# Attention of a fused kernel: where the softmax reciprocals are spread, and how x1 for the residual is made

## The chip, the cores and the metric

The kernel runs on one core of a Trainium2 chip. Time is the device time of one execution in microseconds, the median of several runs. A profile is one execution taken by the hardware profiler; its span runs from the first to the last instruction. The engines are TensorE (PE in the profile; PEld is its loading of weights), VectorE (DVE), ScalarE (ACT), GpSimd (POOL) and SyncE (SP), whose work here is to issue transfers. Each engine works through its own instructions in order. All arithmetic is in float32.

## The reference

Four layers run over 8 sequences (batches) of 512 rows by 512 features: a finite-difference grid step, a transformer layer with conditioning, an expert MLP with layer normalization, and a gated low-rank correction. The change lies in the second, whose attention half is

```python
emb = silu(sin_emb(timestep)) @ W_ada + b_ada
scale, shift = split(emb)                      # one row of 512 each per batch
x = ln(src) * (1.0 + scale) + shift            # x1
q, k, v = x @ Wq + bq, x @ Wk + bk, x @ Wv + bv    # 16 heads of 32
scores = q @ k.T / sqrt(32) + attention_bias   # masked with -inf
ctx = softmax(scores) @ v
x = x + (ctx @ Wo + bo)
```

Softmax is used as exp(s - max) whose weighted sum over v is divided by its own sum. So each of the 16 heads of each row needs one reciprocal, and the residual needs x1 in rows.

## The kernel before, in words

**Stages.** The grid step of batch 0 runs first (to about 75 us of the profile), then attention of all 8 batches with the grid steps of batches 1 to 7 woven in (to about 1105 us), then the MLP stage. A tile has 128 partitions; the 512 rows of a batch are taken as 4 groups r of 128 rows, the 512 features as 4 chunks c of 128, which are 4 heads each.

**Units.** Attention is a loop (L1124 on) over 128 units (b, c, r): batch, four heads, 128 rows. Within a batch t = 4c + r counts them from 0 to 15. Three units are in work at once: `now` gets its softmax, `old` (one unit back) has its weights turned by 128x128 transposes on TensorE (`turned`, L1032), and for `two` (two units back) `values` (L1055) multiplies with v, once per two row groups. `scores` (L1003) of the next unit come last. The order on each engine is the order in which this loop records the calls; `pin` fixes it. Loads that are not pinned can be placed elsewhere by the scheduler.

**Filling.** Between these steps `fill` (L927) gives each t some other matmuls: projections q and k of this batch (t = 0, 1, 4, 5, 8, 9), the output projection `o_block` of the batch before (t = 2, 3, 6, 7), and from t = 9 on the first work of the next batch: `x1_in` (L601) turns its normalized rows `xt` by TensorE and applies scale and shift, which in the turned form are one number per partition; then q, k, v of it. `x1_back` (L617) makes rows of x1 again: four transposes (tile `xb`, PSUM) and an add of `bo` on VectorE (L622), into `xt`. It runs at t = 11 to 14, for batch 0 at t = 2, 3, 4 and 7. `o_block` later adds the attention's result to `xt`.

**Softmax and its division.** `softmax` (L1014) adds the scores to the negative bias and takes the minimum in one VectorE instruction, and ScalarE's exponential leaves the sums, `sums`, 4 heads per unit. At the end of each unit `inverse` (L1070) takes the reciprocal of `old`'s sums on VectorE and ScalarE copies each over the 32 features of its head (`rw`, 128x128). When two's r is 3 (t = 5, 9, 13, and t = 1 of the next batch), `divide` (L1077) turns the four `rw` tiles on TensorE (tile `rb`), ScalarE copies the result out of PSUM (`rbs`), and VectorE multiplies `ctx` by it into `ct` (L1087). PSUM tag `tr`, two buffers, is shared by `turned`, `x1_in`, `x1_back` and `divide`.

**Queues.** SP issues nearly all loads in program order, each after the buffers it writes are free. `load_bias` (L982) brings a unit's bias three units ahead, two halves of 512 KB; GpSimd adds the mask to it (`add_mask`, L994, line L998) one unit ahead. `grid_loads` (L729) brings coefficients and rows for the grid step of a later batch; most of their bytes come at t = 6 and 7. `grid_gate` (L741) makes GpSimd wait, once a unit, until VectorE's last grid operation is done. `x1d` stores a batch's finished rows (1 MB) at t = 9 of the next batch. `rows32` and `spread` (L1415, L1429) of the MLP stage already move rows through DRAM: VectorE transposes 32x32 blocks, one transfer writes them (`td`), eight reads bring them back in another order.

Of the kernel before, what the change touches and what calls it, by code (L numbers as in the profile page):

```python
# [11 lines left out]
F32 = mybir.dt.float32  # L12
# [4 lines left out]
ALU = mybir.AluOpType  # L17
# [3 lines left out]
NB = 8  # L21
S = 512
D = 512
P = 128
R = 4
NH = 16
HD = 32
FF = 2048
NJ = FF // P
KC = D // P  # L30
RK = 32
# [8 lines left out]
def fused_kernel(ctx: ExitStack, tc: tile.TileContext, a: dict):  # L40
    nc = tc.nc

    const = ctx.enter_context(tc.tile_pool(name="const", bufs=1))
    small = ctx.enter_context(tc.tile_pool(name="small", bufs=4))
    xp = ctx.enter_context(tc.tile_pool(name="xp", bufs=1))


    ident = const.tile([P, P], F32, name="ident")
# [116 lines left out]
    w = {}  # L165
# [30 lines left out]
    def load_late():  # L196
# [3 lines left out]
    wl3 = const.tile([P, KC, RK], F32, name="wl3")  # L200
    x1d = [dram.tile([P, R, D], F32, name=f"x1d_{b}") for b in range(NB)]
    first = attention_stage(
        tc, a, small, xp, xt, x_home, x1d, grid, ident, sc1, shift, io, wo8, w, (bqk, bvc, bo),
        g2, mhalf, load_w, load_late,
    )
    mlp_stage(tc, a, small, xp, io, wo8, x1d, ident, eidx, sigs, layernorm, rstd_of, phalf, wl3, g2, b1, first)
# [336 lines left out]


def attention_stage(
    tc, a, small, xp, xt, x_home, x1d, grid, ident, sc1, shift, io, wo8, w, rows,
    g2, mhalf, load_w, load_late,
):

# [9 lines left out]
    with ExitStack() as ctx:  # L559
# [9 lines left out]
        def tp(out, src):  # L569
            pin(nc.tensor.transpose(out, src, ident))  # L570
# [46 lines left out]
        def x1_back(b, r):  # L617
            tr = ps.tile([P, KC, P], F32, name=f"xb_{b}_{r}", tag="tr", bufs=2)
            for c in range(KC):
                tp(tr[:, c, :], x1s[b, c][:, r::R])  # L620
            pin(
                nc.vector.tensor_tensor(  # L622
                    xt[b][:, r, :], tr.rearrange("p c f -> p (c f)"), bo, ALU.add
                )
            )

        def block(out, lhsT, rhs):

# [298 lines left out]
        def fill(b, t):  # L927

            n = b + 1
            jobs = []  # L930
            if b == 0:
                if t == 0:
                    homes = (("m", 1), ("tr", 2), ("tr", 2), ("ctx", 1))
                    for m in range(4):
                        jobs.append(v_block(0, m, *homes[m]))
                        jobs.append(grid_early(j) for j in (m + 3,))
                    jobs.append(grid_early(7) for _ in range(1))
                    jobs.append(mask_out(0, r) for r in (2, 3))
                elif t == 1:
                    jobs.append(add_bv() for _ in range(1))  # L940
                elif t in (2, 3, 4, 7):
                    jobs.append(x1_back(0, (2, 3, 4, 7).index(t)) for _ in range(1))
            if n == NB:
                if t == 0:
                    head["fill"] = halves(b)
                jobs.append(
                    next(head["fill"], None)
                    for _ in range({0: 2, 7: 2, 8: 2, 11: 2, 12: 2, 13: 0, 14: 2, 15: 0}.get(t, 1))
                )
            elif t in (0, 4, 8):  # L950
                jobs.append(q_block(b, t // 4 + 1))
            elif t in (1, 5, 9):
                turn = (lambda c: x1_in(n, c)) if t == 9 else None
                jobs.append(k_block(b, t // 4 + 1, turn=turn))
            elif t in (2, 3, 6, 7):
                if b:
                    jobs.append(o_block(b - 1, (2, 3, 6, 7).index(t)))
            elif t == 11:
                jobs.append(q_block(n, 0))
            elif t == 13:  # L960
                jobs.append(k_block(n, 0))
            else:
                jobs.append(v_block(n, (10, 12, 14, 15).index(t)))
            if n < NB:
                if t in (11, 12, 13, 14):
                    jobs.append(x1_back(n, t - 11) for _ in range(1))
                if t >= 12:
                    jobs.append(load_mask(n, t - 12) for _ in range(1))
            elif t == 8:
                jobs.append(head_stats() for _ in range(1))  # L970
            elif t in (10, 11):
                jobs.append(head_norm(r) for r in (2 * t - 20, 2 * t - 19))
            elif t in (13, 15):
                jobs.append(head_turn(c) for c in (t - 13, t - 12))
            for j in jobs:
                yield from j
# [26 lines left out]
        def scores(b, c, r):  # L1003
            for i in range(4):
                s = ps.tile([P, S], F32, name=f"s_{b}_{c}_{r}_{i}", tag=f"s{i}")
                o = i * HD
                mm(
                    s, qs[b, c][o : o + HD, r * P : (r + 1) * P], ks[b, c][o : o + HD, :],
                    True, True,
                )  # L1010
                ss[i] = s
            sums[b, c, r] = pp.tile([P, 4], F32, name=f"sums_{b}_{c}_{r}", tag="sums", bufs=8)

        def softmax(b, c, r, u):  # L1014

            bt = bias[b, c, r, u]
            for i in range(2):
                h = 2 * u + i
                mn = small.tile([P, 1], F32, name=f"mn_{b}_{c}_{r}_{h}", tag=f"mn{h}")
                pin(  # L1020
                    nc.vector.tensor_tensor_reduce(  # L1021
                        bt[:, i, :], ss[h], bt[:, i, :], -1.0, 3.0e38, ALU.add, ALU.min, mn
                    )
                )
                pin(
                    nc.scalar.activation(  # L1026
                        bt[:, i, :], bt[:, i, :], AF.Exp, bias=mn, scale=-1.0,
                        accum_out=sums[b, c, r][:, h : h + 1],
                    )
                )  # L1030

# [35 lines left out]
                        k == 0, k == KC - 1,  # L1067
                    )

        def inverse(b, c, r):  # L1070
            rs = small.tile([P, 4], F32, name=f"rs_{b}_{c}_{r}", tag="rs")
            pin(nc.vector.reciprocal(rs, sums.pop((b, c, r))))
            rw = pp.tile([P, 4, HD], F32, name=f"rw_{b}_{c}_{r}", tag="rw", bufs=4)
            pin(nc.scalar.copy(rw, rs[:, :, None].to_broadcast([P, 4, HD])))
            sums["w", b, c, r] = rw

        def divide(b, c):  # L1077
            rb = ps.tile([P, R, P], F32, name=f"rb_{b}_{c}", tag="tr", bufs=2)
            for r in range(R):
                tp(rb[:, r, :], sums.pop(("w", b, c, r)).rearrange("p h d -> p (h d)"))  # L1080
            rbs = pp.tile([P, S], F32, name=f"rbs_{b}_{c}", tag="rbs", bufs=1)
            pin(nc.scalar.copy(rbs, rb.rearrange("f r p -> f (r p)")))

            tag, bufs = (("gq", 2), ("gc", 3))[c // 2] if b == NB - 1 else ("ct", 5)
            ct = pp.tile([P, S], F32, name=f"ct_{b}_{c}", tag=tag, bufs=bufs)
            pin(
                nc.vector.tensor_tensor(  # L1087
                    ct, ctxs.pop((b, c)).rearrange("f r p -> f (r p)"), rbs, ALU.mult
                )
            )  # L1090
            cts[b, c] = ct

        def drain(jobs):
            for _ in jobs:
                pass
# [28 lines left out]
        for i in range(n + 2):  # L1124
            now = units[i] if i < n else None
            old = units[i - 1] if 1 <= i <= n else None
            two = units[i - 2] if i >= 2 else None
            jobs = fill(now[0], 4 * now[1] + now[2]) if now else iter(())
            grid_gate(i)
            if i + 1 < n:  # L1130
                add_mask(*units[i + 1])
            grid_step(i - 1, grid_pow)
            pair = two and two[2] % 2 == 1
            if pair:
                values(two[0], two[1], two[2] // 2)
            for u in range(2):
                if old:
                    turned(*old, u)
                if now:
                    softmax(*now, u)  # L1140
                next(jobs, None)
            drain(jobs)
            split = pair and two[2] == R - 1
            if split:
                grid_step(i, lambda n, j: grid_sums(n, j, late=False))
                divide(two[0], two[1])
            if old:
                inverse(*old)
            if i + 3 < n:
                load_bias(*units[i + 3])  # L1150
            if now and now[0] and now[1:] == ((2, 1) if now[0] < NB - 1 else (3, 3)):
                nc.sync.dma_start(x1d[now[0] - 1], xt[now[0] - 1])
            if now and now[0] == NB - 1:
                head_load(4 * now[1] + now[2])
            grid_step(i, lambda n, j: grid_sums(n, j, early=not split))
            grid_step(i, grid_loads)
            if i + 1 < n:
                scores(*units[i + 1])
# [893 lines left out]
```

## Time and profile before

| | |
|---|---|
| Time, median of 3 runs | 2699.4 us (2698.77 to 2700.58) |
| Profiled execution, its own time | 2699.88 us |
| Span of that profile | 2698.1 us |
| Busy: PE, DVE, POOL, ACT | 2659.8, 1925.3, 1479.1, 1009.5 us |
| `tr` transposes (L570) in 75 to 1080 us | x2016, 277 ns each |
| `rb`, `xb` transposes (L570) there | x124 at 278 ns, x128 at 284 ns |
| `rw` copies (L1074, ACT) there | x126 at 292 ns |
| `rbs` copies (L1082, ACT) there | x31 at 571 ns |
| `rs` reciprocals (L1072, DVE) there | x126 at 168 ns |
| Mask additions (L998, POOL) there | x254 at 2140 ns |

How to read the lines shown below: a group has line, engine, operation, tile written and tiles read, sizes, how many, then busy time and mean ns of one, then idle time before them and what ended it. A timeline line has its start and length in us. Several instructions of a kind that follow each other are one line. Neighbouring matmuls overlap in the records, so their starts tell more than their lengths.

### The profile page before, as it was taken

How to read it: one execution, taken by the hardware profiler on the slowest of the kernel's cores; microseconds unless marked ns; L12 is line 12 of the kernel's file. 1: busy time of each engine (PE TensorE's matmuls, PEld its weight loads, DVE VectorE, ACT ScalarE, POOL GpSimd, SP SyncE). 2: the span in 40 equal slices, each digit the busy share in tenths (PEclk: the TensorE clock that was granted, in tenths of full speed). 3: DMA queues.
4: the chain of work that ended last, by engine and by line, in shares of the span. 5: the costliest groups of instructions: out<-in, count | busy, mean ns of one | idle time of the engine just before them, and what ended most of it. 6: DMA issues, size and time to landing. Idle time of an engine off the chain costs nothing.

```text
span 2698.1 us, 39602 instructions
## 1 busy us (share of the span) xinstructions
PE 2659.8 (99%) x14310; PEld 1972.4 (73%) x14310; DVE 1925.3 (71%) x3602; ACT 1009.5 (37%) x2157; POOL 1479.1 (55%) x1090
## 2 busy tenths in 40 slices
PE   7999999999999999999999999999999999999998
PEld 4455555555555555788888888888888888888887
DVE  7888888888888756576666656656556765666665
ACT  2566767676676766212212211211111211211211
POOL 3455555555555655366566465555555555555553
PEclk9999999999999999999999999999999999999999
DMA  8765757666676544644453553455335445346321
GB/s 310 247 217 179 242 182 245 194 230 220 197 242 193 171 150 137 197 146 115 138 156 98 162 146 100 146 155 152 123 118 184 127 151 190 125 146 199 121 97 45
DMA packets 218720, 451.39 MB, mean 167 GB/s; under 512 B 27192, under 2 KB 54400, under 8 KB 209438
## 3 DMA queue, kind: packets, MB, share of 16 engines
q1 hardware_dynamic: 214714, 438.12, 48.9%
q0 software_dynamic: 3360, 10.68, 2.9%
q8 instruction: 114, 1.87, 0.3%
q14 instruction: 80, 0.66, 0.1%
q10 hardware_dynamic: 452, 0.07, 0.0%
HBM read 390.04 MB, written 54.57 MB: 165 GB/s over the span
## 4 chain that ended last, share of the span: by engine, by line
PE 95%; DVE 3%; DMA 1%; issue 0%; SPq 0%; ACT 0%; ACTq 0%; POOL 0%; DVEq 0%; POOLq 0%
PE u L1195 29%; PE y L1195 29%; PE tr L570 8%; PE s L567 6%; PE ctx L567 5%; PE o L567 4%; PE pq L567 4%; PE pk L567 4%; PE pv L567 4%; PE l L251 1%; PE rb L570 1%; PE xb L570 1%; DVE x L697 0%; DMA a<-in_A 0%; DVE bt L1021 0%
## 5 line engine op out<-in xcount | busy, mean ns | idle before, releaser
L998 POOL TENSOR_TENSOR bt<-bt,mk 128x1024 f32<-128x1024 f32 x256 | 542.4, 2140 | 58.2 <-DMA bt<-in_bias 52.5
L1195 PE MATMUL y<-wo,act 128*128 128x256 f32 x2560 | 566.5, 380 | 0.0
L1195 PEld LDWEIGHTS y<-wo,act 128*128 128x128 f32 x2560 | 484.4, 190 | 71.9 <-issue 6.7
L1026 ACT ACTIVATE bt<-bt,mn 128x512 f32<-128x512 f32 x512 | 365.7, 716 | 81.4 <-DVE mn L1021 80.5
L570 PEld LDWEIGHTS tr<-ident,bt 128*128 128x128 f32 x2048 | 228.7, 141 | 145.4 <-issue 113.5
L1021 DVE CUSTOM_DVE_ANT_0 bt<-s,bt 128x512 f32<-128x512 f32 x512 | 330.8, 683 | 1.3 <-PE s L567 1.3
L1195 PE MATMUL u<-bt,wi 128*128 128x256 f32 x1440 | 330.5, 379 | 0.0
L1201 DVE TENSOR_TENSOR act<-u,u 128x512 f32<-128x512 f32 x256 | 173.1, 684 | 200.8 <-PE u L1195 132.6
L1195 PEld LDWEIGHTS u<-bt,wi 128*128 128x128 f32 x1440 | 273.5, 190 | 37.2
L570 PE MATMUL tr<-ident,bt 128*128 128x128 f32 x2048 | 274.2, 277 | 4.2 <-DVE x L622 1.7
L1195 PE MATMUL u<-tb,ws 128*128 128x256 f32 x1024 | 242.2, 379 | 0.0
L1053 ACT COPY pt<-tr 128x512 f32<-128x512 f32 x306 | 172.9, 582 | 158.8 <-PE tr L570 155.6
L1195 PE MATMUL y<-t,s 128*128 128x256 f32 x1024 | 227.8, 380 | 0.0
L1204 POOL TENSOR_TENSOR t<-wo,t 128x512 f32<-128x512 f32 x64 | 107.3, 1700 | 203.1 <-PE y L1195 203.1
L1051 DVE COPY pt<-tr 128x512 f32<-128x512 f32 x206 | 141.7, 688 | 107.4 <-PE tr L570 99.2
L1195 PEld LDWEIGHTS u<-tb,ws 128*128 128x128 f32 x1024 | 194.3, 190 | 26.6 <-DVE tb L1201 0.2
L1195 PEld LDWEIGHTS y<-t,s 128*128 128x128 f32 x1024 | 194.0, 190 | 26.1
L1559 ACT ACTIVATE act<-act,b 128x512 f32<-128x512 f32 x128 | 82.9, 711 | 293.0 <-DVE act L1201 293.0
L1559 ACT ACTIVATE act<-act,bi 128x512 f32<-128x512 f32 x128 | 83.8, 712 | 282.6 <-DVE act L1201 282.6
L1578 ACT COPY u<-u 128x512 f32<-128x512 f32 x64 | 36.4, 569 | 391.3 <-PE u L1195 273.1
L567 PE MATMUL s<-kt,qt 32*128 32x512 f32 x1024 | 177.1, 642 | 1.8 <-DVE mn L1021 0.9
L1201 DVE TENSOR_TENSOR x<-y,x 128x512 f32<-128x512 f32 (+1 forms) x97 | 64.7, 680 | 154.0 <-PE y L1195 103.6
(326 smaller groups left out, 4229.2 us busy)
## 6 DMA issues: line engine op xcount, KB each, us to landing
bt<-in_bias SPq DMA_DIRECT2D x256, 512.0 KB
wo<-in_W SPq DMA_DIRECT2D x32, 1024.0 KB
wi<-in_Wi SPq DMA_DIRECT2D x32, 1024.0 KB
wo<-in_Wo_e SPq DMA_DIRECT2D x32, 1024.0 KB
wi<-in_W SPq DMA_DIRECT2D x28, 1024.0 KB
td<-tt SPq DMA_DIRECT2D x22, 1024.0 KB
bt<-td SPq DMA_DIRECT2D x176, 128.0 KB
gq<-coef_q SPq DMA_DIRECT2D x21, 512.0 KB
```

The costliest lines, as they stand in the source:

```text
L567: pin(nc.tensor.matmul(out, lhsT=lhsT, rhs=rhs, start=start, stop=stop))
L570: pin(nc.tensor.transpose(out, src, ident))
L998: nc.gpsimd.tensor_tensor(bt, bt, mask[b, r][:, None, :].to_broadcast([P, 2, S]), ALU.add)
L1021: nc.vector.tensor_tensor_reduce(bt[:, i, :], ss[h], bt[:, i, :], -1.0, 3.0e38, ALU.add, ALU.min, mn)
L1026: nc.scalar.activation(bt[:, i, :], bt[:, i, :], AF.Exp, bias=mn, scale=-1.0, accum_out=sums[b, c, r][:, h : h + 1],)
L1051: pin(nc.vector.tensor_copy(pt[:, :, r % 2, :], tr))
L1053: pin(nc.scalar.copy(pt[:, :, r % 2, :], tr))
L1195: pin(nc.tensor.matmul(out, lhsT=lhsT, rhs=rhs, start=start, stop=stop))
L1201: pin(nc.vector.tensor_tensor(out, x, y, op))
L1204: pin(nc.gpsimd.tensor_tensor(out, x, y, op))
L1559: nc.scalar.activation(acts[g][:, k, :], acts[g][:, k, :], func, bias=bi[:, j : j + 1])
L1578: pin(nc.scalar.copy(u1, p[0]))
```

## The change

Reciprocals: sums of all four units of (b, c) go to one tile of 4 heads by 4 row groups. After the fourth, one reciprocal writes 32 columns (the 16 twice), VectorE transposes them in 32x32 blocks, SP writes 16 KB to DRAM and reads it back four times with broadcast, so that each head's row of 512 reciprocals lies on its 32 partitions. `divide` multiplies by that tile, with its columns taken in the order in which they lie. `inverse` is called when old's r is 3, ahead of the rest of the unit's filling; `divide` stays where it was, one unit later.

x1 of batches 1 to 7: once, at t = 5 and 6 of batch 0, `rows_out` turns scale (which already holds the 1) and shift by four transposes each, adds `bo` to the second and stores them as rows in DRAM. At t = 8 `rows_in` brings the next batch's two rows, broadcast to 128 partitions; the second goes to `bo` itself. GpSimd multiplies (t = 10 to 13) and VectorE adds (t = 11 to 14), in place on the normalized rows. Batch 0 keeps `x1_back`.

```diff
+        ghd = dram.tile([2, NB, D], F32, name="ghd")
+        rows1 = {}
+        def rows_out(i):
+            tr = ps.tile([NB, KC, P], F32, name=f"gh_{i}", tag="tr", bufs=2)
+            for c in range(KC):
+                tp(tr[:, c, :], (sc1, shift)[i][:, c, :])
+            t = pp.tile([NB, D], F32, name=f"ghs_{i}", tag="ct", bufs=5)
+            v = tr.rearrange("b c f -> b (c f)")
+            if i:
+                pin(nc.vector.tensor_tensor(t, v, bo[0:NB, :], ALU.add))
+            else:
+                pin(nc.vector.tensor_copy(t, v))
+            pin(nc.sync.dma_start(ghd[i], t))
+        def rows_in(n):
+            rows1[n] = pp.tile([P, D], F32, name=f"gh_{n}", tag="gh", bufs=1)
+            for i, t in enumerate((rows1[n], bo)):
+                pin(nc.sync.dma_start(t, ghd[i, n : n + 1, :].to_broadcast([P, D])))
+        def x1_scale(n, r):
+            v = xt[n][:, r, :]
+            pin(nc.gpsimd.tensor_tensor(v, v, rows1[n], ALU.mult))
+        def x1_shift(n, r):
+            v = xt[n][:, r, :]
+            pin(nc.vector.tensor_tensor(v, v, bo, ALU.add))
...
                 elif t in (2, 3, 4, 7):
                     jobs.append(x1_back(0, (2, 3, 4, 7).index(t)) for _ in range(1))
+                elif t in (5, 6):
+                    jobs.append(rows_out(t - 5) for _ in range(1))
...
             if n < NB:
+                if t == 8:
+                    jobs.append(rows_in(n) for _ in range(1))
+                if t in (10, 11, 12, 13):
+                    jobs.append(x1_scale(n, t - 10) for _ in range(1))
                 if t in (11, 12, 13, 14):
-                    jobs.append(x1_back(n, t - 11) for _ in range(1))
+                    jobs.append(x1_shift(n, t - 11) for _ in range(1))
...
-            sums[b, c, r] = pp.tile([P, 4], F32, name=f"sums_{b}_{c}_{r}", tag="sums", bufs=8)
+            if r == 0:
+                sums[b, c] = pp.tile([P, 4, R], F32, name=f"sums_{b}_{c}", tag="sums", bufs=3)
...
-        def inverse(b, c, r):
-            rs = small.tile([P, 4], F32, name=f"rs_{b}_{c}_{r}", tag="rs")
-            pin(nc.vector.reciprocal(rs, sums.pop((b, c, r))))
-            rw = pp.tile([P, 4, HD], F32, name=f"rw_{b}_{c}_{r}", tag="rw", bufs=4)
-            pin(nc.scalar.copy(rw, rs[:, :, None].to_broadcast([P, 4, HD])))
-            sums["w", b, c, r] = rw
+        rd = [dram.tile([P, RK], F32, name=f"rd_{i}") for i in range(2)]
+        def inverse(b, c):
+            rs = pp.tile([P, 2, NH], F32, name=f"rs_{b}_{c}", tag="rs", bufs=2)
+            sm = sums.pop((b, c)).rearrange("p h r -> p (h r)")
+            pin(nc.vector.reciprocal(rs, sm[:, None, :].to_broadcast([P, 2, NH])))
+            rt = pp.tile([P, 2 * NH], F32, name=f"rt_{b}_{c}", tag="rt", bufs=2)
+            pin(nc.vector.transpose(rt, rs.rearrange("p u x -> p (u x)")))
+            d = rd[c % 2]
+            pin(nc.sync.dma_start(d, rt))
+            rbs = sums["b", b, c] = pp.tile([P, S], F32, name=f"rbs_{b}_{c}", tag="rbs", bufs=1)
+            rows = d.rearrange("(a u h r) j -> u h a (r j)", u=2, h=4, r=R)[0]
+            for h in range(4):
+                pin(
+                    nc.sync.dma_start(
+                        rbs[h * HD : (h + 1) * HD, :].rearrange("d (a x) -> d a x", x=P),
+                        rows[h : h + 1].to_broadcast([HD, P // RK, P]),
+                    )
+                )
 
         def divide(b, c):
-            rb = ps.tile([P, R, P], F32, name=f"rb_{b}_{c}", tag="tr", bufs=2)
-            for r in range(R):
-                tp(rb[:, r, :], sums.pop(("w", b, c, r)).rearrange("p h d -> p (h d)"))
-            rbs = pp.tile([P, S], F32, name=f"rbs_{b}_{c}", tag="rbs", bufs=1)
-            pin(nc.scalar.copy(rbs, rb.rearrange("f r p -> f (r p)")))
+            rbs = sums.pop(("b", b, c))
...
                 nc.vector.tensor_tensor(
-                    ct, ctxs.pop((b, c)).rearrange("f r p -> f (r p)"), rbs, ALU.mult
+                    ct.rearrange("f (r a j) -> f r a j", r=R, j=RK),
+                    ctxs.pop((b, c)).rearrange("f r (a j) -> f r a j", j=RK),
+                    rbs.rearrange("f (a r j) -> f r a j", r=R, j=RK), ALU.mult,
                 )
...
                 next(jobs, None)
+            if old and old[2] == R - 1:
+                inverse(*old[:2])
             drain(jobs)
             split = pair and two[2] == R - 1
             if split:
                 grid_step(i, lambda n, j: grid_sums(n, j, late=False))
                 divide(two[0], two[1])
-            if old:
-                inverse(*old)
```

In the built program SP's stores of `x1d` stand, at t = 8, between the write of the reciprocals and their reads.

More of the change, by code (lines that the diff above doesn't have):

```diff
@@ L202, in fused_kernel @@
     first = attention_stage(
-        tc, a, small, xp, xt, x_home, x1d, grid, ident, sc1, shift, io, wo8, w, (bqk, bvc, bo),
+        tc, a, small, dram, xp, xt, x_home, x1d, grid, ident, sc1, shift, io, wo8, w, (bqk, bvc, bo),
         g2, mhalf, load_w, load_late,
@@ L545, in attention_stage @@
 def attention_stage(
-    tc, a, small, xp, xt, x_home, x1d, grid, ident, sc1, shift, io, wo8, w, rows,
+    tc, a, small, dram, xp, xt, x_home, x1d, grid, ident, sc1, shift, io, wo8, w, rows,
     g2, mhalf, load_w, load_late,
@@ L1027, in softmax @@
                         bt[:, i, :], bt[:, i, :], AF.Exp, bias=mn, scale=-1.0,
-                        accum_out=sums[b, c, r][:, h : h + 1],
+                        accum_out=sums[b, c][:, h, r : r + 1],
                     )
```

## The prediction

> **What bounds the kernel now.** I read the page's engine sums and its chain first, then one batch of the attention stage by windows, then the timeline of the places that the diff touches.
>
> ```profile
> PE 2659.8 (99%) x14310; PEld 1972.4 (73%) x14310; DVE 1925.3 (71%) x3602; ACT 1009.5 (37%) x2157; POOL 1479.1 (55%) x1090
> PE u L1195 29%; PE y L1195 29%; PE tr L570 8%; PE s L567 6%; PE ctx L567 5%; PE o L567 4%; PE pq L567 4%; PE pk L567 4%; PE pv L567 4%; PE l L251 1%; PE rb L570 1%; PE xb L570 1%; DVE x L697 0%; DMA a<-in_A 0%; DVE bt L1021 0%
> ```
>
> TensorE sets the time; the removed transposes (`rb`, `xb`) stand in its chain with about 1% each. One batch of attention:
>
> ```profile
> core 0: us, PE busy (x) PEld busy (x) DVE busy (x) ACT busy (x) POOL busy (x), PEclk, DMA share, GB/s
> 502.22:628.00 125.78, 125.53 (x817) 69.19 (x816) 109.84 (x236) 87.59 (x209) 71.59 (x52) 1.00 0.65 212
> ```
>
> TensorE is full (125.5 of 125.8 us), VectorE second with 109.8 (87%), so about 16 us of TensorE's time could go before VectorE's sum binds. The edit takes under 5 a batch. The clock is 1.00 here and gives nothing.
>
> **What leaves TensorE.** The groups say how many; a duration of 277 ns overlaps its neighbours, so I price a removal by starts of neighbours with and without it.
>
> ```profile
> L570 PE MATMUL xb<-ident,x 128*128 128x128 f32 x128 | 20.7, 284 | 1.0 <-ACT pt L1053 1.0
> L570 PE MATMUL rb<-ident,rw 128*128 128x128 f32 x124 | 19.2, 278 | 1.8 <-DVE pt L1051 1.0
> ```
> ```profile
> 508.68 1.88 PE L567 MATMUL pk<-x,Wk 128*128 128x512 f32 x4
> 510.39 0.60 PE L570 MATMUL rb<-ident,rw 128*128 128x128 f32 x4
> 510.93 1.14 PE L567 MATMUL s<-kt,qt 32*128 32x512 f32 x8
> ...
> 517.33 2.27 PE L567 MATMUL s<-kt,qt 32*128 32x512 f32 x8
> ...
> 548.92 1.88 PE L567 MATMUL pv<-Wv,x 128*128 128x512 f32 x4
> 550.74 1.14 PE L567 MATMUL s<-kt,qt 32*128 32x512 f32 x8
> ...
> 557.19 1.88 PE L567 MATMUL pq<-x,Wq 128*128 128x512 f32 x4
> 558.91 0.63 PE L570 MATMUL xb<-ident,x 128*128 128x128 f32 x4
> 559.47 1.14 PE L567 MATMUL s<-kt,qt 32*128 32x512 f32 x8
> ```
>
> Without either, projection to scores takes 550.74 - 548.92 = 1.82 us. With `rb` 2.25, so 0.43 each; with `xb` 2.28, so 0.46 each. Of 32 divides, 31 lie in the flow: 13.3 us. `x1_back` stays for batch 0, so 28 go: 12.9 us.
>
> **A second gain, on VectorE.** The scores at 517.33 take 2.27 us where others take 1.14: TensorE waits 1.13 us for late VectorE. What made it late in that unit:
>
> ```profile
> 510.26 1.22 DVE L697 TENSOR_TENSOR ga<-ga,gf 128x1024 f32<-128x1024 f32 x1
> 512.37 0.69 DVE L1087 TENSOR_TENSOR ct<-ctx,rbs 128x512 f32<-128x512 f32 x1 [0.88 <-ACT rbs L1082]
> ```
>
> `divide` waits 0.88 us for ScalarE's copy of `rb`. With `rbs` loaded early that wait goes, and one small reciprocal (0.09 start to start): 0.97 instead of 0.43, so 0.54 more. It recurs at t = 1 and t = 5 while the grid work of a next batch is there, 13 times: 7.0 us. Gains together: 33.2.
>
> **What is added, and where it lies.**
> - `rows_out`: two sets of four transposes on TensorE at 0.54 (the `rb` slot): 1.1 us, once.
> - VectorE loses 128 reciprocals (start to start 0.09: 11 us) and 28 `x1_back` adds, and gets 32 reciprocals, 32 transposes of 128x32 and 28 `x1_shift` adds. The new small ones I put at 0.17 each, as the reciprocal's row has it (a 128x512 transpose takes 0.70): 32 x 0.34 = 11. A wash.
> - ScalarE loses 128 copies `rw` and 32 `rbs`. It is 70% busy in the batch; I count nothing beyond the 0.88 above.
> - GpSimd gets 28 `x1_scale`, 1.1 us by half of L998's 2.14, up to 1.7 by L1204's 128x512. They follow the mask addition of the next unit and lie in GpSimd's idle time (43% of the batch); `x1_shift` comes one unit later.
> - `x1_shift` now reads two SBUF tiles where `x1_back` read PSUM. The row: a VectorE product that starts while the mask addition runs to 551.4 takes 1.88 instead of 1.22.
>
> ```profile
> 550.60 1.88 DVE L697 TENSOR_TENSOR gc<-gc,gf 128x1024 f32<-128x1024 f32 x1
> ```
>
> [...] By the row, 0.66. But VectorE's 0.7 us wait for `xb` before each add (18.3 us over 23, L622) goes, so I take 0, with ends -7 and +7 on the path.
>
> **The round trip through DRAM.** SP, in program order, gets per block of four heads: a 16 KB write that waits for VectorE, then four 64 KB reads that wait for the write; the bias, grid and mask loads of that unit stand behind them. `rows_in` adds two 256 KB broadcasts to seven units (t = 8). In all 12 MB more on a queue that moves 27 MB a batch; it is their place that counts. Nearest are the same steps of the MLP stage: 1 MB out, then reads with as many pieces (128, of 1 KB; here 512 B).
>
> ```profile
> 1175.47 0.34 SPq L1432 DMA_DIRECT2D td<-tt  x1
> 1179.33 3.66 SPq L1439 DMA_DIRECT2D bt<-td  x8
> 1184.05 0.81 ACT L1461 ACTIVATE bt<-bt,g 128x512 f32<-128x512 f32 x1 [17.93 <-DMA bt<-td]
> ```
>
> Write: 1179.33 - 1175.81 = 3.5 us, of which 1.05 MB at 384 GB/s (the window below) are 2.7, leaving 0.8 for a small one. Reads: 4.7 from first issue to use. With 0.35 on VectorE and 0.4 of issue: 6.3 us. [...] Time available, from the end of the softmax of t = 4 (502.07) to where `ct` could begin (511.4): 9.3 us; t = 0 to 1 has 9.4, t = 12 to 13 about 10. [...]
>
> [...]
>
> ```profile
> 527.69 1.13 SPq L714 DMA_DIRECT2D gq<-coef_q  x2
> 535.71 1.23 DVE L697 TENSOR_TENSOR gq<-gq,gf 128x1024 f32<-128x1024 f32 x1 [0.40 <-DMA gq<-coef_q]
> ...
> 535.70:541.00 5.30, 5.30 (x39) 3.35 (x29) 4.68 (x10) 3.14 (x8) 3.99 (x3) 1.00 1.03 384
> ```
>
> The second `gq` landed 7 us after its issue. From 527.7 to 535.7 some 2.0 MB moved (254 GB/s), so about 0.6 MB beyond the 1.4 that `gq` needed. Ahead of the small write stand two bias halves, `x` and `gc`, 2.1 MB, of which 1.5 remain: 3.9 us at 384 GB/s, until 539.6. [...] `ct` can begin at 544.8: VectorE waits 0.3 to 3 us. I take 2, nearer the upper end because `x1d` does stand there in the built program's order; VectorE has 0.5 to give (its wait at 548.7), so TensorE loses 1.5 six times: 9 us. If all is hidden, 0. The bias halves behind land about 4 us before the softmax that uses them (GpSimd adds the mask at 547.2, VectorE reads at 555.1); that cover gone would cost what they are late.
>
> [...]
>
> **The sum**, against the profiled execution of 2699.9 (span 2698.1 and 1.8 around it): 33.2 - 1.1 - 9.0 - 2.3 = 20.8, so 2679.1; it stood 0.5 over the runs' median of 2699.4, so 2679.
>
> **Rivals.** (1) All four round trips hidden: 29.8 gained, 2670; with whole slots saved (0.54 and 0.56) 2663. For it: 0.3 us is the lower end of that wait. [...] (3) On the other side: the wait at t = 9 is long. Six batches, each costing (wait - 0.5); with 29.8 to lose the sign turns at 5.5 us of wait, reads landing after 550.3. At 7 us it costs 39, time 2709. For it: DMA share 1.01 from 533 to 544, and `x1d` between write and reads; against: the backlog counted gives 548 at the latest. That the edit does nothing is excluded, since 240 transposes leave a full engine.
>
> **Chances.** Forecast case (wait of 1 to 3 us) 0.50, hidden 0.20, the middle 0.12, long wait 0.18. A measurement of this kernel tells about 0.2% (5.4 us) from no change; half of the middle case lies within it, with the tails of its neighbours: faster 0.73, same 0.09, slower 0.18. The forecast's own range is 2670 to 2687. The range for eight in ten goes from 2663 to 2705, leaving out most of case 3.
>
> **What would show it.** Groups `rb` gone and `xb` x16; a batch of 121 to 123 us; the long scores at t = 1 and 5 back near 1.3 us; `ct` waiting on DMA only at t = 9, by 1 to 3 us, in six batches; the first `o` block waiting some 4 us at the end of attention; the MLP stage as before. Wrong if `ct` waits on DMA at all t, if GpSimd waits for bias inside batches 1 to 5, or if a batch stays at 125.8.

## The result, and the profile after

The changed kernel takes 2711.7 us (median of 5 runs, 2707.7 to 2715.6) against 2699.4 (5 runs, 2698.8 to 2702.4): ratio 1.0045, 95% interval 1.0033 to 1.0056. It is 12.3 us slower, where 20 us faster was forecast. The profiled execution took 2707.7 us, the shortest of its runs, with a span of 2705.8: 7.7 us over the span before, so the trace can account for 7.7 of the 12.3 us.

The engine sums and the chain that ended last, from the page of the changed kernel:

```profile
PE 2638.5 (98%) x14078; PEld 1941.9 (72%) x14078; DVE 1979.6 (73%) x3540; ACT 960.1 (35%) x1997; POOL 1529.3 (57%) x1118
PE 82%; DVE 8%; DMA 6%; SPq 1%; issue 1%; ACT 1%; POOL 0%; ACTq 0%; DVEq 0%; POOLq 0%
PE u L1243 29%; PE y L1243 28%; PE tr L570 6%; PE s L567 4%; PE o L567 4%; PE ctx L567 3%; PE pq L567 3%; DVE bt L1057 2%; PE pk L567 2%; DMA rd<-rt 2%; DVE x L726 2%; PE pv L567 2%; DMA mu<-in_mask 1%; DVE pt L1087 1%; PE l L251 1%
```

TensorE is busy 21.3 us less than before, as the edit promised; the span is longer all the same, so about 29 us of TensorE's time are new idle time. The chain, which was TensorE almost alone, now goes through VectorE (8%) and through two transfers: the 16 KB write `rd` and the mask load `mu`. The chain of the kernel before, by engine:

```profile
PE 95%; DVE 3%; DMA 1%; issue 0%; SPq 0%; ACT 0%; ACTq 0%; POOL 0%; DVEq 0%; POOLq 0%
```

Where in a batch? The starts of the scores of each unit t, after minus before, say it. Over t = 0 to 10 each of batches 1 to 6 gains 2.8 us (batch 3: from 5.45 behind to 2.60 behind). From t = 10 to the next t = 0, batches 0 to 5 lose 5.9, 4.7, 4.0, 4.1, 3.8 and 4.1 us; batch 6, which prepares no grid step, gains 0.8. At the end of attention the kernel is 5.3 us behind, the last divide makes it 7.7, and the MLP stage keeps that to the end. Engine busy times, first over one batch's length (from t = 5 of batch 3, as in the batch line of the prediction, with its columns), then over t = 10 to 15 of batch 3 alone:

```profile
506.63:633.64 127.01, 122.17 (x786) 64.70 (x785) 117.67 (x229) 81.04 (x189) 78.94 (x56) 1.00 0.67 223
546.93:597.35 50.42, 45.72 (x290) 23.65 (x289) 47.99 (x88) 28.00 (x67) 33.58 (x22) 1.00 0.71 233
```

The same stretch, t = 10 to 15, of the kernel before:

```profile
544.33:590.67 46.34, 46.34 (x309) 26.16 (x308) 39.63 (x92) 30.75 (x75) 26.23 (x18) 1.00 0.66 211
```

TensorE was full there with 46.34 of 46.34 us. Now VectorE is busy 47.99 of 50.42 us, 8.4 more than before with four instructions fewer, and TensorE waits.

What VectorE's instructions cost there, from its groups between 200 and 960 us (batches 1 to 5), after:

```profile
L726 DVE TENSOR_TENSOR x<-x,gq 128x1022 f32<-128x1022 f32 x22 | 39.2, 1784 | 0.2
L654 DVE TENSOR_TENSOR x<-x,bo 128x512 f32<-128x512 f32 x24 | 33.5, 1397 | 0.0
L726 DVE TENSOR_TENSOR x<-x,gg 128x1024 f32<-128x1024 f32 x12 | 21.8, 1815 | 0.0
L726 DVE TENSOR_TENSOR e<-e,e 128x8 f32<-128x8 f32 x10 | 14.4, 1437 | 0.3
```

and before:

```profile
L697 DVE TENSOR_TENSOR x<-x,gq 128x1022 f32<-128x1022 f32 x22 | 26.4, 1201 | 0.2
L622 DVE TENSOR_TENSOR x<-xb,bo 128x512 f32<-128x512 f32 x25 | 17.2, 689 | 13.6 <-PE xb L570 13.6
L697 DVE TENSOR_TENSOR x<-x,gg 128x1024 f32<-128x1024 f32 x11 | 14.9, 1352 | 0.0
L697 DVE TENSOR_TENSOR e<-e,e 128x8 f32<-128x8 f32 x10 | 1.7, 167 | 0.3
```

The add of `bo` takes 1.40 us instead of 0.69, the grid's product `x<-x,gq` 1.78 instead of 1.20, and a product of 128x8 elements, `e<-e,e`, 1.44 instead of 0.17. These instructions handle as many elements as before; they stand and wait. What for shows when they are sorted by what GpSimd does meanwhile. Before, none of the 22 `x<-x,gq` met a mask addition, and each took 1.19 to 1.22 us. After, the 12 that met neither a mask addition nor `x1_scale` took 1.21 to 1.23 us, the 10 that met one 2.28 to 3.14. The adds of the kernel before, which read one operand from PSUM (`xb`), took 0.68 to 0.69 us each, 4 of the 25 with a mask addition beside them. So what waits is VectorE's work with both operands in SBUF, beside GpSimd's work on SBUF; the texts below call this "ports", which is a name alone: what the two engines share is not shown. The timelines of batch 3 show it. VectorE:

```profile
548.70 0.69 DVE L1133 TENSOR_TENSOR ct<-ctx,rbs 128x512 f32<-128x512 f32 x1 [0.51 <-DMA rbs<-rd]
...
555.31 3.85 DVE L726 TENSOR_TENSOR e<-e,e 128x8 f32<-128x8 f32 x2
...
564.53 1.77 DVE L654 TENSOR_TENSOR x<-x,bo 128x512 f32<-128x512 f32 x1
566.22 2.28 DVE L726 TENSOR_TENSOR x<-x,gq 128x1022 f32<-128x1022 f32 x1
```

GpSimd in the same time:

```profile
554.90 4.23 POOL L1033 TENSOR_TENSOR bt<-bt,mk 128x1024 f32<-128x1024 f32 x2 [4.11 <-DMA bt<-in_bias]
559.09 2.32 POOL L650 TENSOR_TENSOR x<-x,gh 128x512 f32<-128x512 f32 x1
...
561.53 4.22 POOL L1033 TENSOR_TENSOR bt<-bt,mk 128x1024 f32<-128x1024 f32 x2
565.71 1.71 POOL L650 TENSOR_TENSOR x<-x,gh 128x512 f32<-128x512 f32 x1
```

`e<-e,e` ends at 559.16, when the mask addition ends (559.13). The add of `bo` begins at 564.53 while the next mask addition runs, and ends at 566.30, 0.6 us after it; `x<-x,gq`, issued behind it, stands while `x1_scale` runs until 567.4, and ends 1.1 us later, nearly the 1.2 it takes alone. In the kernel before, `grid_gate` kept the two engines mostly apart: a mask addition began when VectorE's last grid operation was done, ran while VectorE read scores from PSUM, and was over before most of its next grid work. At t = 12 of batch 3 `x<-x,gq` ended at 561.65, the mask addition ran from 561.88 to 566.1, and the next `x<-x,gq` began at 567.14. GpSimd there:

```profile
561.73 0.19 POOL L746 TENSOR_TENSOR gate<-x 128x1 f32<-128x1 f32 x1 [2.62 <-DVE x L697]
561.88 4.23 POOL L998 TENSOR_TENSOR bt<-bt,mk 128x1024 f32<-128x1024 f32 x2
```

Two things broke that. `x1_scale` stands behind the mask additions and runs into the grid work. And the mask addition of t = 10 comes late, here by 4.11 us of waiting for bias. SP's queue shows why:

```profile
536.95 0.32 SPq L1116 DMA_DIRECT2D rd<-rt  x1
537.31 0.43 SPq L1200 DMA_DIRECT2D x1d<-x  x1
544.04 2.63 SPq L1121 DMA_DIRECT2D rbs<-rd  x4
546.71 0.43 SPq L646 DMA_DIRECT2D gh<-ghd  x1
547.18 0.43 SPq L646 DMA_DIRECT2D bo<-ghd  x1
547.72 3.22 SPq L1022 DMA_DIRECT2D bt<-in_bias  x4
```

SP stands for 6.3 us, from the store to the first read, until the write has landed; then come the four reads and two row loads, and only then the bias. It takes both: GpSimd waits for bias once in each of batches 1 to 5, 4.1 to 5.6 us each time; before it did so in none of them, and in two runs below, one without the row loads and one with them elsewhere, its waits there are under 1 us each. `ct` itself waits 0.51 us. Who else waits, over the whole span, after (us in total, times, longest):

```profile
POOL bt L1033 <- DMA bt<-in_bias: 78.7, 15, 11.6
ACT mk L593 <- DMA mu<-in_mask: 49.8, 14, 4.7
```

and before:

```profile
POOL bt L998 <- DMA bt<-in_bias: 52.5, 28, 9.4
ACT mk L593 <- DMA mu<-in_mask: 3.5, 1, 3.5
```

ScalarE waits for masks 14 times: once at the start, as before, twice in each of batches 0 to 5, once in batch 6. At t = 12 the first mask load of the next batch stands in SP's queue behind the write and the reads of the third divide. Batch 3, after:

```profile
557.76 4.85 SPq L1022 DMA_DIRECT2D bt<-in_bias  x2
572.68 0.34 SPq L1116 DMA_DIRECT2D rd<-rt  x1
574.12 1.75 SPq L1121 DMA_DIRECT2D rbs<-rd  x4
575.91 0.43 SPq L588 DMA_DIRECT2D mu<-in_mask  x1
```

and before:

```profile
557.91 0.47 SPq L588 DMA_DIRECT2D mu<-in_mask  x1
```

Here SP stands 10.1 us, from 562.61 to 572.68, until VectorE has made the reciprocals that the write takes, and 1.1 us more until the write has landed. So at t = 12 it is the write's own wait for VectorE, much more than its landing, that makes the mask late; at t = 8 it is the landing. SP's waits for the two, from 200 to 1080 us:

```profile
SPq L1116 <- DVE rt L1114: 184.6, 28, 11.2
SPq L1121 <- DMA rd<-rt: 64.5, 28, 7.2
```

ScalarE stands in `mk` (4.5 us in batch 3), the copies `pt` of turned weights stand behind `mk`, and TensorE behind those (0.94 us in batch 3, until 579.30).

### The profile page after: what moved, and what is told of

Its sections match the earlier page's. It is cut to its first block, busy times and chain, and to the rows that moved or that the text cites. A ratio compares the mean times of both kernels' runs of the same rounds, so it can differ in the third digit from the quotient of the medians.

```text
span 2705.8 us, 39209 instructions
## 1 busy us (share of the span) xinstructions
PE 2638.5 (98%) x14078; PEld 1941.9 (72%) x14078; DVE 1979.6 (73%) x3540; ACT 960.1 (35%) x1997; POOL 1529.3 (57%) x1118
## 4 chain that ended last, share of the span: by engine, by line
PE 82%; DVE 8%; DMA 6%; SPq 1%; issue 1%; ACT 1%; POOL 0%; ACTq 0%; DVEq 0%; POOLq 0%
PE u L1243 29%; PE y L1243 28%; PE tr L570 6%; PE s L567 4%; PE o L567 4%; PE ctx L567 3%; PE pq L567 3%; DVE bt L1057 2%; PE pk L567 2%; DMA rd<-rt 2%; DVE x L726 2%; PE pv L567 2%; DMA mu<-in_mask 1%; DVE pt L1087 1%; PE l L251 1%
## 5 line engine op out<-in xcount | busy, mean ns | idle before, releaser
L1033 POOL TENSOR_TENSOR bt<-bt,mk 128x1024 f32<-128x1024 f32 x256 | 545.3, 2154 | 90.2 <-DMA bt<-in_bias 78.7
L570 PE MATMUL tr<-ident,bt 128*128 128x128 f32 x2048 | 277.9, 277 | 33.5 <-DVE pt L1087 21.3
```

The lines of the kernel that those rows point to most:

```text
L1033: nc.gpsimd.tensor_tensor(bt, bt, mask[b, r][:, None, :].to_broadcast([P, 2, S]), ALU.add)
```

## The experiments

Theory A, ports: `x1_scale`, and the mask additions that it pushes back, run beside VectorE's work on SBUF. Theory B, queue: SP, held until the write has landed, makes bias late. Four runs (the kernel before took 2699.3 us beside them).

**The reciprocals alone** (`rows_out` goes too).

```diff
-                if t == 8:
-                    jobs.append(rows_in(n) for _ in range(1))
-                if t in (10, 11, 12, 13):
-                    jobs.append(x1_scale(n, t - 10) for _ in range(1))
-                if t in (11, 12, 13, 14):
-                    jobs.append(x1_shift(n, t - 11) for _ in range(1))
+                if t in (11, 12, 13, 14):
+                    jobs.append(x1_back(n, t - 11) for _ in range(1))
```

> The reciprocals go through DRAM as in the change, the residual's x1 is turned back by TensorE as before. Theory A (ports: GpSimd's x1_scale and the mask additions that it pushes back run beside VectorE's work on SBUF, and one waits for the other): without x1_scale the loss of about 4 us in each of six batches after t = 10 is gone and the gain up to t = 10, 2.85 us a batch, stays: about 2682 us, batch 3 about 122.9 us. Theory B (queue: SP stands behind the four reads at t = 8 until the write has landed, bias comes late, the mask addition then runs beside the grid work of t = 10 and 11): the loss stays for its larger part, 2693 to 2702 us, and the second product of the ghost columns still takes over 3 us instead of 0.2.

Measured: 2699.9 us, ratio 0.9998 (0.9989 to 1.0007). Not A: without `x1_scale` the gain is still gone, and the gain of 2.85 us a batch up to t = 10 is there, as foreseen. The time lies in B's range, but by luck: B's sign failed, `e<-e,e` is back at 0.17 us. B named only bias, but most of the loss lies between t = 13 and t = 15, 12.5 us over seven batches, and there it is the mask. ScalarE and then TensorE of this run, batch 1:

```profile
321.23 0.63 ACT L593 ACTIVATE mk<-mu 128x512 bf16<-128x512 uint8 x1 [6.37 <-DMA mu<-in_mask]
321.76 0.57 ACT L1082 COPY pt<-tr 128x512 f32<-128x512 f32 x1
```
```profile
322.38 0.91 PE L570 MATMUL tr<-ident,bt 128*128 128x128 f32 x4 [2.14 <-ACT pt L1082]
323.09 3.35 PE L567 MATMUL pk<-x,Wk 128*128 128x512 f32 x4
```

**The row vectors alone**: the kernel before with `rows_out`, `rows_in`, `x1_scale` and `x1_shift` in place of the 28 `x1_back`; `inverse` and `divide` as before.

> The row vectors make x1 as in the change, the reciprocals stay on TensorE and ScalarE as before. Theory A: the loss after t = 10 stays, about 4 us in six batches, without the gain of the reciprocals: 2715 to 2725 us. Theory B: no reads hold SP up, so the loss is gone and the 28 transposed sets are gained: 2688 us.

Measured: 2703.3 us, ratio 1.0014 (1.0005 to 1.0023). Neither: less than A foresaw, but the 11.8 us that 28 transposed sets less two new ones should bring are gone and 4 more. No read holds SP here (`e<-e,e` 0.17 us), and `x<-x,gq` takes 1.66 us, `x<-x,gg` 1.88, the add of `bo` 1.22. So the row vectors have a price of their own, of about 16 us. The ports are in it (`x<-x,gq` took 1.20 us before); how much of it they are this run doesn't show, since the row loads are in SP's queue as well.

**x1_scale by VectorE.**

```diff
-            pin(nc.gpsimd.tensor_tensor(v, v, rows1[n], ALU.mult))
+            pin(nc.vector.tensor_tensor(v, v, rows1[n], ALU.mult))
```

> The change with x1_scale done by VectorE instead of GpSimd. Theory A: VectorE gets four more instructions of about 0.6 us a batch and loses four or more waits of about 1 us: x<-x,gq back at 1.2 us, time 2698 to 2706 us, below the change. Theory B: nothing is won and 2.4 us of work a batch are added: 2716 us or more.

Measured: 2719.6 us, ratio 1.0068 (1.0054 to 1.0081). `x<-x,gq` is back at 1.21 us as A said, the time is not; it is what B gave (2716 or more). VectorE's work now stands ahead of the unit's first `pt` copy at t = 11, where bias is late and the mask addition meets the small products. VectorE and TensorE of this run, batch 3 (the mask addition ran from 557.09 to 561.3):

```profile
555.43 0.69 DVE L650 TENSOR_TENSOR x<-x,gh 128x512 f32<-128x512 f32 x1
...
557.16 2.11 DVE L783 TENSOR_TENSOR m<-gab,gf 128x16 f32<-128x16 f32 x1
...
559.29 2.10 DVE L783 TENSOR_TENSOR m<-gab,gf 128x16 f32<-128x16 f32 x1
```
```profile
563.99 1.94 PE L570 MATMUL tr<-ident,bt 128*128 128x128 f32 x8 [2.70 <-DVE pt L1087]
```

**The reads behind the unit's bias and grid loads.**

```diff
             grid_step(i, grid_loads)
+            if old and old[2] == R - 1:
+                reads(*old[:2])
```

> The change with the four reads of the reciprocals issued at the end of their unit, behind the unit's bias and grid loads, instead of ahead of them. Theory A: bias and mask addition come in time at t = 10, the ghost columns' product is back at 0.2 us and 1 to 2 us a batch are won, the rest of the loss stays: about 2702 us. Theory B: the loss is gone: about 2687 us. Either way ct may wait longer for its reads at t = 9.

Measured: 2722.2 us, ratio 1.0084 (1.0070 to 1.0098). Both forecasts missed (2702 and 2687). `e<-e,e` is back at 0.17 us, so the held queue had its part in making it wait. But the bias loads wait for buffers, and the reads now wait behind them: `ct` stands 20 times, 41.7 us in all. And the write stayed where it was, so SP still stands for VectorE (177.6 us from 200 to 1080) and ScalarE for masks (15 times, 30.6 us). Reads on this queue are either in somebody's way or late themselves.

**Theory C** says what the first four runs left: the reads hold SP, and the mask load at t = 12 is the dearest victim. For the runs on it the kernel before took 2699.5 us, in later ones 2699.7.

The masks one unit earlier, in the full change and in the reciprocals alone:

```diff
                 if t >= 12:
-                    jobs.append(load_mask(n, t - 12) for _ in range(1))
+                    jobs.append(mask_out(n, t - 12) for _ in range(1))
+                if 11 <= t < 15:
+                    jobs.append(mask_in(n, t - 11) for _ in range(1))
```

> The change with each mask row block of the next batch loaded one unit earlier, at t = 11 to 14 instead of 12 to 15; ScalarE still turns it into mk at t = 12 to 15. Theory C (the reads hold SP until the write has landed; at t = 12 the mask load stands behind them, ScalarE stands in mk with the copies of turned weights behind it, and TensorE waits for those): ScalarE's waits in mk fall from 50 us to under 10 and the time falls by 5 to 12 us, to 2700 to 2707 us. Theory A (ports of GpSimd and VectorE alone): no change, 2711 us.

> The reciprocals through DRAM alone (x1 turned back by TensorE), with the mask loads one unit earlier. Theory C: the jumps of TensorE between t = 13 and t = 15, 12.5 us over seven batches in the trace of the reciprocals alone, go: about 2687 us. If the mask was only the wait that ended last and bias takes its place: 2695 to 2700 us.

Measured: the full change 2702.2 us, 1.0009 (1.0000 to 1.0018); the reciprocals alone 2682.7 us, 0.9940 (0.9927 to 0.9952). ScalarE's waits for masks fall to 2.9 and 2.5 us, once. C holds for the victim: the load moved by one unit, ahead of the write, is worth 9.5 us in the change and 17.1 in the reciprocals alone, where t = 13 to 15 goes from 12.5 us lost to 3.1 gained. Of what holds SP there, C named the smaller part: the landing, and not the write's wait for VectorE. The same move in the kernel before:

> The kernel before with the masks loaded one unit earlier and nothing else. ScalarE waited 3.5 us, once, for a mask there, so by theory C nothing changes: 2699 us. If an earlier mask load is a gain of its own: below 2694 us.

Measured: 2699.3 us, 0.9999 (0.9990 to 1.0008). So the gain is that of a wait which the change had made.

The write on ScalarE's queue, without and with early masks:

```diff
-            pin(nc.sync.dma_start(d, rt))
+            pin(nc.scalar.dma_start(d, rt))
```

> The reciprocals through DRAM alone, with the 16 KB write issued on ScalarE's queue instead of SP's. If the write lands late because it stands in SP's own queue behind 2 MB of loads, it now lands in 2 to 3 us at t = 8 instead of 8, SP is held that much less, the mask addition of t = 10 comes early again and some 4 us of jumps after t = 11 go: about 2695 us. If the engines' load makes it late, whatever the queue: 2700 us, reads issued 8 us after the write as before.

> The reciprocals through DRAM alone, with the mask loads one unit earlier and the write on ScalarE's queue. If the two causes are separate, both gains: about 2683 us. If the write on the other queue lands no earlier: 2687 us, as with the masks alone.

Measured: 2698.6 us, 0.9999 (0.9990 to 1.0007), and 2686.4 us, 0.9953 (0.9940 to 0.9966), 3.6 more than with early masks alone. Another queue doesn't make the write land earlier: at t = 8 of batch 3 the reads are issued 8.67 us after the write (531.88 to 540.55) in the first of these runs, 8.85 in the reciprocals alone. And SP isn't freed: it now stands at the reads for both, for the reciprocals and for the landing, where it stood 175.0 + 64.5 us in the reciprocals alone:

```profile
SPq L1114 <- DMA rd<-rt: 262.2, 29, 11.9
```

Why the landing is as late from this queue the run doesn't show.

The store of the last batch's rows, put at t = 11 instead of between write and reads, on top of the early masks:

```diff
-            if now and now[0] and now[1:] == ((2, 1) if now[0] < NB - 1 else (3, 3)):
-                nc.sync.dma_start(x1d[now[0] - 1], xt[now[0] - 1])
+            if now and now[0] and now[1:] == ((2, 3) if now[0] < NB - 1 else (3, 3)):
+                pin(nc.sync.dma_start(x1d[now[0] - 1], xt[now[0] - 1]))
```

> The reciprocals through DRAM with early masks (2682.7 us), with the 1 MB store of the last batch's rows put at t = 11 instead of between the write and the reads at t = 8. If the store holds the reads or the bias behind it: ct's waits at t = 9 shorter by up to 2.7 us, six times, of which the jumps of TensorE at t = 11 (some 4 us in all) are the part that shows: 2679 us. If the loads ahead of the write are what makes it late: 2683 us.

Measured: 2679.6 us (2679.2 to 2680.1), 0.9927 (0.9913 to 0.9940): 20.1 us under the kernel before, as forecast if the store is in the way, and the best of all. Its page, sums and chain:

```profile
PE 2640.3 (99%) x14182; PEld 1956.7 (73%) x14182; DVE 1932.1 (72%) x3538; ACT 964.3 (36%) x1997; POOL 1482.1 (55%) x1090
PE 91%; DVE 5%; DMA 2%; ACT 1%; issue 1%; SPq 0%; POOL 0%; ACTq 0%; DVEq 0%; POOLq 0%
```

TensorE is back in the chain with 91%. Between 200 and 960 us `ct` waits 1.2 us for the reads and GpSimd 29.0 for bias; with the store in its old place these were 3.5 and 16.2 us, so the move makes the reads earlier and the bias later. Now the other half of the change. With early masks it still costs 2702.2 - 2682.7 = 19.5 us, and by the transposes it should win 11.8. One of its two instructions was left out at a time, so that x1 is not scaled, or not shifted:

> The change with early masks (2702.2 us), without GpSimd's 28 products x1_scale: x1 is then not multiplied. Theory A (ports): the product itself and the mask additions that it pushes back are what VectorE waits for; the adds of bo and the grid products x<-x,gq and x<-x,gg are back at 0.7 and 1.2 us, and the 28 sets of transposes are won: about 2672 us. Theory D (VectorE's adds on SBUF and the row loads are the price, not GpSimd's product): 2690 us or more.

> The change with early masks (2702.2 us), without VectorE's 28 adds x1_shift: x1 is then not shifted. Theory A: GpSimd's products still collide with the grid products, which keep a mean of about 1.7 us; VectorE has 28 adds of 0.7 us less: 2685 to 2695 us. Theory D: 2672 us.

Measured: 2683.9 us, 0.9940 (0.9926 to 0.9953), and 2685.4 us, 0.9946 (0.9933 to 0.9960). Leaving out either wins 17 to 18 us, so the prices don't add. A is right about the grid products (without `x1_scale` `x<-x,gq` takes 1.21 us, without `x1_shift` 1.68) and about the time without `x1_shift`, wrong about the time without `x1_scale`: 2684 is not 2672. Without `x1_scale`, `e<-e,e` still takes 1.60 us and the add of `bo` 1.00, so the late mask addition is not `x1_scale`'s doing. Both runs keep the row loads. VectorE's busy time from t = 10 to 15 of batch 3 puts these runs in order: 47.0 of 50.7 us with both, 45.6 of 47.2 without `x1_shift`, 43.1 of 46.8 without `x1_scale`, 41.8 of 47.7 with neither (there TensorE, with its 16 `xb` more, is busy 47.2). That VectorE's fullness is why the two cost so much together is argued; the next run, with 48.1 of 49.4 us and a shorter time, doesn't fit the order.

What else stood before bias at t = 8? The full change with early masks and the late store, and the same with the row loads moved:

```diff
-                if t == 8:
+                if t == (2 if b else 8):
                     jobs.append(rows_in(n) for _ in range(1))
```

> The full change with early masks and with the 1 MB store at t = 11, everything that SP holds up repaired, x1 still made by x1_scale and x1_shift. If what is left of the loss is VectorE's time between t = 10 and t = 15 (GpSimd's product and VectorE's adds on SBUF): it stays, 2696 to 2702 us, some 20 us above the same repairs with x1 turned back (2679.6 us), VectorE over 46 of 50 us busy there. If the store was behind it: under 2690 us.

> As the run beside it (early masks, store at t = 11), with the two row loads of 256 KB put at t = 2 instead of t = 8, from batch 1 on. If the row loads, which stand ahead of the bias at t = 8, make the mask addition late so that it meets the grid's small products at t = 10: those are back under 0.7 us, and 6 to 14 us are won, 2685 to 2695 us. If the row loads don't matter: as the run beside it, 2696 to 2702 us.

Measured: 2699.8 us, 1.0002 (0.9993 to 1.0011), and 2689.5 us, 0.9963 (0.9949 to 0.9976). Two row loads of 256 KB a batch, six units earlier from batch 1 on, are worth 10.3 us, and `e<-e,e` is back at 0.17 us. So the first stayed at 2699.8 not by VectorE's work alone, as its forecast had it. Part of the collision goes to the product `m` before it (1.09 us against 0.56), so the mask addition still meets VectorE, but earlier and for less. What remains over 2679.6 is 9.9 us, with `x<-x,gq` at 1.71 and `x<-x,gg` at 1.82 us. The ports are the likely cause, but not shown to be all of it: in the trace, whose execution was the longest of its five (2692.9 us), 7.3 of the 13.6 us of difference arise in batch 0, where the row loads still come at t = 8 and TensorE ran slower twice: behind a wait of 1.90 us, ended at 93.47, eight `pb` matmuls took 5.40 us (3.70 in the kernels before and after the change), and behind one of 2.82 us, ended at 181.75, four `pq` took 3.57 instead of 1.88. As estimates from these runs: with the 10.3 us of the row loads taken out, one of the two instructions alone costs 2.7 us (`x1_shift`) or 4.2 (`x1_scale`) beyond the 11.8 it should win, both together about 22.

In a row, from the change: early masks -9.5, late store -2.4, early row loads -10.3, x1 turned back by TensorE -9.9: from 2711.7 to 2679.6.

## Why the prediction was wrong

- **What leaves TensorE: right.** A `rb` slot and the wait behind it, forecast 0.43 + 0.54 = 0.97 us, measured 0.43 + 0.61, at t = 1 and again at t = 5. The scores after the second, batch 3 of the changed kernel, 1.67 us instead of 2.27:

```profile
513.09 1.88 PE L567 MATMUL pk<-x,Wk 128*128 128x512 f32 x4
514.90 1.14 PE L567 MATMUL s<-kt,qt 32*128 32x512 f32 x8
...
521.31 1.67 PE L567 MATMUL s<-kt,qt 32*128 32x512 f32 x8
```

  The list of signs had said near 1.3. The first projection to its scores takes 1.81 us, where it took 2.25 with `rb`. `xb` at 0.46: four of them and one `rb` make 2.3 us, which is what batch 6 gains from t = 10 to 15 without `x1_scale`.
- **The wait of `ct` at t = 9: place and times right, size too big.** Batch 3 is 3.37 us behind there. Less that, the reads are issued at 540.7 and used at 545.3, and VectorE is ready at 544.8, as forecast. So the wait is 0.5 us, within "0.3 to 3"; "I take 2" was the mis-sized term, and with it the 9 us. The changed kernel shows no wait of 2 us there, and none of 3; the longest of batches 0 to 5 is 1.26 us, in batch 0. In batches 1 to 5 `ct` waits three times, 1.8 us in all, and t = 9 gains 0.77 us where 1.5 - 0.43 were to be lost. The estimate of 0.8 us for the small write was too low: in batch 3 from its issue to that of the reads it took 1.4 us at t = 12, and 7.1 at t = 8 with loads ahead of it.
- **What stands behind the round trip: failed.** I set the round trip (6.3 us) against the time until `ct` needs it (9.3 us at t = 4 to 5), and for `ct` it does end in time there: at t = 1, 5 and 13 of batches 0 to 6 `ct` waits for no read. The price lies with those who stand in SP's queue behind the write and the reads. The text named "the bias, grid and mask loads of that unit", and that the write "waits for VectorE", and then gave a price to none: only bias was looked at, and only for the softmax that reads it 4 us later. Put at nothing: the mask load at t = 12, held 10.1 us by the write's wait and 1.1 by its landing, with ScalarE and the `pt` copies behind it (9.5 us in the change, 17.1 in the reciprocals alone), and the mask addition of GpSimd, which came in time for the softmax but beside VectorE's grid products. The two row loads, counted as bytes ("it is their place that counts"), got no price for their place: 10.3 us. The sign of being wrong, GpSimd waiting for bias inside batches 1 to 5, came true in all five.
- **"I take 0, with ends -7 and +7" failed**, for `x1_shift` and `x1_scale`. The waits for `xb` that go (18.3 us over 23 is 0.8 each, not 0.7) brought TensorE nothing that shows; the waits that come fill VectorE in the one stretch where it has little left. Also, I counted waits of the add alone and not of the grid products behind it. Measured: 4 us lost by the row vectors alone instead of 11.8 won, so about 16; 9.9 and 11.8, so about 22, in the repaired change. Both figures hold more than the ports, and what the ports cost alone is not shown. The one row I had for them (0.66 us) was too small: `x1_shift` took 0.71 us more on the mean (1.40 instead of 0.69), and the 10 `x<-x,gq` beside GpSimd 1.1 to 1.9 us more.
- **"about 16 us of TensorE's time could go before VectorE's sum binds"** rested on an average. From t = 10 to 15 it was 46.3 - 39.6 = 6.7 us, and 8.4 were added there.
- **The last divide: right**, 2.3 us in the sum. How the 2.3 comes about no run shows; measured is when its product begins, 1100.18 instead of 1092.49: less the 5.27 us that attention was behind, 2.4. MLP: right, nothing.
- **The rivals.** The long wait at t = 9 had the sign, by a mechanism that didn't occur (0.5 us there in batch 3). The held queue was in none of them. That the best version ends at 2679.6, the number forecast, is luck: it has no row vectors, which were to win 11.8 us, and loses almost nothing at t = 9, where 9 were to be lost.

## What to carry to other kernels

A transfer that waited for an engine or for another transfer held those behind it in its queue: SP stood 10.1 us at t = 12, and the mask load put ahead of that was worth 17.1 us in the reciprocals alone. So go through the queue's next entries one by one, name the engine that waits for each and what stands behind it there, and move what isn't urgent ahead. Where a gate made two engines take turns, a late arrival of one cost the other, though the data was in time for its reader: bias late by 4.11 us, and two `e<-e,e` took 3.85 us instead of 0.37. Read free time from the stretch in which the new work falls, and try a half of the change at a time: here one half, with the mask loads and the store put elsewhere in the queue, wins 20 us, and the other half takes it back.

## What the hardware showed beyond that

TensorE's clock fell after some short waits. In the traces of all kernels here, between 200 and 1085 us, 12 of 23 idle gaps of 1.9 to 3.0 us were followed by a lower granted clock (a mean of 0.50 to 0.72 over the next 3 us), and one of 74 gaps of 0.9 to 1.9 us was. Each fall is to 0.50, for 3.4 us or twice that; four came without such a gap. Busy times by windows of the reciprocals alone, around the gap of 2.14 us above (the last but two column is the clock):

```profile
320.00:322.00 2.00, 0.24 (x3) 0.01 (x1) 1.72 (x4) 0.77 (x2) 1.63 (x1) 1.00 0.66 140
322.00:324.00 2.00, 1.62 (x6) 1.10 (x7) 0.19 (x2) 2.00 (x6) 0.00 (x0) 0.66 0.93 320
324.00:326.00 2.00, 2.00 (x4) 0.84 (x3) 0.00 (x0) 1.64 (x5) 0.00 (x0) 0.50 0.93 314
```

The projection there took 3.35 us instead of 1.88: the wait of 2.14 us cost 3.6. So a wait of about 2 us was followed by a fall in about half of the cases; what decides it is not shown. In the changed kernel it was one of three: 2.06 and 2.56 us were not followed by one, 2.27 us (ended at 695.65) by a clock of 0.50 from 696.0 to 699.4.

Two tiny instructions waited longer than a large one: `e<-e,e`, two products of 128x8 elements, took 3.85 us beside a mask addition (`x<-x,gq`, 128x1022, 2.28 beside `x1_scale`), and 0.37 alone (`x1_scale` by VectorE, batch 3).
